# Two products moved in the hand-written order of a two-layer graph network: V's second and G's fourth

## The chip, the cores and the metric

The kernel runs on one core of a Trainium2 chip. The time is the device time of one execution in microseconds (us). The core has five engines with a queue of instructions each: PE (TensorE, matrix products), DVE (VectorE), ACT (ScalarE), POOL (GpSimd) and SP (SyncE, which here only issues DMAs). An engine works through its queue in order; where an instruction needs what another engine makes, or a buffer that another engine still reads, it waits on a semaphore, and all that is behind it in its queue waits too.

## The reference

The input `x` has 128 sets of 128 rows of 512 numbers, all float32. Two layers follow one another on it:

```python
# layer 0
h = jnp.maximum(_layernorm(x, axis=-1), 0.0)
x = x + _L0_gnn_ref(h, adj, L0_gnn_Wq, L0_gnn_Wk, L0_gnn_Wv)
# layer 1
h = jnp.maximum(_layernorm(x, axis=-1), 0.0)
x = x + _L1_gnn_ref(h, adj, L1_gnn_Wq, L1_gnn_bq, L1_gnn_Wk, L1_gnn_bk, L1_gnn_Wv, L1_gnn_bv)
```

Layer 0 makes `q`, `k` and `v` by three products with 512x512 weights, then `rel = adj.T * (q k^T)`, divides each row of `rel` by its norm, and returns `rel v`. Layer 1 is attention with 8 heads of 64: scores `q k^T / 8`, a mask from `adj`, softmax over each row, and the product with `v`.

## The kernel before

**Groups and layers.** Four of the 128 sets form a group (`G = 4`), so there are 32 groups. `run` (L707) goes through a list of step names, written out by hand, and calls each step in turn. A cycle of the main loop (L735 to L740) handles several groups at different stages at once: `m` is the group in layer 0, `n` the same group as it enters layer 1, `l` the group before it in layer 1, `p` and `o` those before that, `f` the next group, whose inputs are fetched. The lists are `FIRST` (cycle 0, L673), `SECOND` (cycle 1, L680), `ORDER` (cycles 2 to 31, L689: 30 cycles) and `LAST` (L699). The scheduling is manual (L720), so each engine gets its instructions in just the order in which the steps issue them.

**Products by seven.** Each big product (512 rows of a group by a 512x512 weight) is made as a 2x2 block product with seven block products instead of eight. `Product` (L202) has them as `P1` to `P7`. In layer 0 there are two: `G`, which takes the place of q and k together (`h` times the product of their weights), and `V`. In layer 1 there are `Q`, `K` and `V`. One `P` step issues four matmul calls, which are eight matmuls in the trace (x8 in a row), followed by one instruction of ACT or DVE that takes the result out of the accumulator memory (PSUM):

- `P1` fills bank "x"; ACT copies it out (`keep`).
- `P2` fills bank "y"; DVE adds it to what P1 left (`add`, L250).
- `P5` fills bank "z"; ACT copies it out.
- `P6` accumulates on "x"; ACT copies it out.
- `P3` accumulates on "z"; DVE adds it (`add`).
- `P7` accumulates on "x"; DVE adds it (`add`).
- `P4` accumulates on "x"; ACT copies it out.

So one bank x carries P1, P6, P7 and P4 in turn, and each time the result is read out before the next product accumulates on it. `V` of layer 1 uses DVE for all of them (`copy` with a bias row, L243). The names in the profile are `pg` (G), `pv` (V of both layers), `pq`, `pk`, with `_x`, `_y`, `_z` for the bank.

**Banks.** The banks of all products, and `po` of `A` (L625), come from one pool of four (`ps_mm`, L61). A bank is free for the next tile when the last reader of its old tile is done. V's "y" of layer 0 is special: after P2 is read out, `N` (L415) writes the row norms into the same bank, and `norms` (L425) reads them, so this bank stays taken from `m.V.P2` to `m.norms`.

**Inputs of the products.** `T` (L319) turns a half of `h` on DVE from what a DMA brought back (`u_h`). `sumA` and `sumB` (L357, L368) make the sums `s` of the blocks on DVE; G.P5 needs the first of them, and P6, P3 and P7 the others. `R` (L388) multiplies G's result with `h`, `mask_rel` applies the adjacency on DVE.

**The order around the change, in ORDER.** DVE's queue in this stretch holds `m.T1`, the two sums of `m.sumA`, `p.wt3` (a reciprocal and a transpose, L515 and L517), the two sums of `m.sumB`, the add of `m.G.P2`, those of `m.G.P3` and `m.G.P7`, `o.ot1` (L651: two transposes and two multiplications, whose results POOL adds to `out` by DMA), the add of `m.V.P2`, and the statistics of the next group (`f.stat0` to `f.stat3`). PE's queue holds K's last products, `m.G.P1`, `l.K.P4`, `m.G.P2`, `m.V.P1`, `m.G.P5`, `m.G.P6`, `m.G.P3`, `m.G.P7`, `m.V.P2`, `m.G.P4`, `m.V.P6`, `m.R`.

**The first two cycles.** FIRST takes group 1 (`f`) through all of G but P4, then turns layer 1's `h` of group 0 (`n.T0`), and SECOND begins with `l.Q.P1`, which needs it, then `m.G.P4` of group 1.

Of the kernel before, what the change touches and what calls it, by code (L numbers as in the profile page):

```python
# [21 lines left out]
def kernel(  # L22
# [352 lines left out]
    class Layer0(Layer):  # L375
        n = 0
# [64 lines left out]
    class Layer1(Layer):  # L441
        n = 1
# [232 lines left out]
        w.scale m.G.P3 m.V.P1 f.hn1 f.rd1 w.sumv m.G.P7 m.V.P2 w.sumq m.G.P4 m.V.P5  # L675
        m.R m.mask_rel m.square f.T0 m.V.P6 m.V.P3 m.N m.norms m.V.P7 m.O0 m.xO0 m.O1 m.xO1 n.stat0 n.stat1
        n.inv0 m.V.P4 n.hn0 n.rd0 f.T1 f.start f.G.P1 f.sumA m.O2 m.xO2 m.O3 m.xO3 n.stat2 n.stat3 n.inv1
        f.G.P5 f.sumB f.G.P6 n.hn1 n.rd1 f.G.P2 f.G.P3 f.G.P7 n.T0 w.sumk n.T1 n.start
    """.split()
    SECOND = """  # L680
        l.Q.P1 m.G.P4 l.sumA l.Q.P2 l.sumB l.K.P1 l.K.P2 l.Q.P5 l.Q.P6 l.sto0 l.sto1 f.load0 f.load1 l.Q.P3 l.K.P5 l.K.P6 l.Q.P7
        l.K.P3 l.K.P7 f.load2 f.load3 l.Q.P4 l.K.P4 m.V.P1 f.stat0 f.stat1 f.inv0
        m.V.P2 m.V.P6 m.R m.mask_rel m.square f.stat2 f.stat3 f.inv1
        l.S0 l.S1 m.N l.mkA1 m.norms m.V.P5 l.exC1 l.mkB1 m.V.P7 l.exD1 l.wr1 l.add_mask0 m.V.P3 l.mx0
# [4 lines left out]
    ORDER = """  # L689
        l.Q.P1 p.mkA3 l.sumA m.hn0 l.Q.P2 p.mkB3 l.K.P1 l.sumB m.rd0 l.K.P2 p.ot0 l.Q.P5 p.exC3 p.wt2 l.Q.P6 p.exD3 p.wr3  # L690
        m.hn1 m.rd1 l.sto0 l.sto1 l.Q.P3 l.Q.P7 m.T0 l.K.P5 l.K.P6 l.Q.P4 o.rdo1 f.load0 f.load1 l.K.P3
        l.K.P7 m.T1 m.sumA p.wt3 m.sumB m.start m.G.P1 l.K.P4 m.G.P2 f.load2 f.load3 m.V.P1 m.G.P5 m.G.P6
        m.G.P3 m.G.P7 o.ot1 m.V.P2 m.G.P4 f.stat0 f.stat1 f.inv0 f.stat2 f.stat3 f.inv1 m.V.P6 m.R m.mask_rel p.A1 m.square
        l.S0 p.oc1 l.S1 m.N l.mkA1 m.norms m.V.P5 l.exC1 l.mkB1 m.V.P7 l.exD1 l.wr1 l.add_mask0 m.V.P3 l.mx0
        m.V.P4 l.ex0 l.wr0 m.O0 m.xO0 m.O1 m.xO1 n.stat0 n.stat1 n.inv0 n.hn0 n.rd0 l.start_v l.V.P1 m.O2 m.xO2 m.O3 m.xO3
        n.stat2 n.stat3 n.inv1 l.V.P2 l.V.P5 n.hn1 n.rd1 l.wt1 l.V.P6
# [23 lines left out]
    with tc.manual_schedule(engines={EN.PE, EN.SP, EN.Pool, EN.DVE, EN.Activation}):  # L720
        o, p, l, m = None, None, None, Layer0(0)
# [9 lines left out]
        f = Layer0(1)  # L731
# [3 lines left out]
        for g in range(NG):  # L735
            n = Layer1(g)
            if g:
                f = Layer0(g + 1) if g + 1 < NG else None
            run((FIRST, SECOND, ORDER)[min(g, 2)], o=o, p=p, l=l, m=m, n=n, f=f, w=Weights1())
            o, p, l, m = p, l, n, f  # L740
# [31 lines left out]
```

## Time and profile before

| what | us |
|---|---|
| median of the runs shown (3) | 2475.11 (2472.4 to 2475.55) |
| the profiled execution | 2480.48 |
| its span, first to last instruction | 2478.7 |
| one cycle of ORDER, from V's P5 of one group to that of the next (1019.74 to 1095.78) | 76.0 |
| one product of eight matmuls, from its start to that of the next | 1.73 |
| an add of DVE from PSUM (L250) | 0.69 |
| a copy of ACT from PSUM (L234) | 0.585 |
| transpose of half of `h` on DVE (L322) | 1.24 |
| all waits of DVE for `u_h` (88 times) | 238.8 |
| waits of DVE for G's bank z, in all (31) and for G's bank x (32) | 69.8 and 32.0 |

Times in the profile count from the start of the span. In rows of the timeline and of the chain of waits the first number is the start and the second the length; x8 is the number of instructions merged into the row, and a bracket gives the idle time of the engine before it with what ended it. Matmuls are pipelined, so a group of eight shows 1.89 us in the timeline although the next begins 1.73 us after it. A window's row has, after its length, the busy time and number of instructions of PE, of PE's weight loads, DVE, ACT and POOL, then the granted clock of TensorE (1.00 is full), the DMA share and GB/s.

### The profile page before, as it was taken

How to read it: one execution, taken by the hardware profiler on the slowest of the kernel's cores; microseconds unless marked ns; L12 is line 12 of the kernel's file. 1: busy time of each engine (PE TensorE's matmuls, PEld its weight loads, DVE VectorE, ACT ScalarE, POOL GpSimd, SP SyncE). 2: the span in 40 equal slices, each digit the busy share in tenths (PEclk: the TensorE clock that was granted, in tenths of full speed). 3: DMA queues.
4: the chain of work that ended last, by engine and by line, in shares of the span. 5: the costliest groups of instructions: out<-in, count | busy, mean ns of one | idle time of the engine just before them, and what ended most of it. 6: DMA issues, size and time to landing. Idle time of an engine off the chain costs nothing.

```text
span 2478.7 us, 40450 instructions
## 1 busy us (share of the span) xinstructions
PE 2464.8 (99%) x14688; PEld 2117.4 (85%) x14688; DVE 1684.5 (68%) x2739; ACT 1012.4 (41%) x3248; POOL 375.9 (15%) x692
## 2 busy tenths in 40 slices
PE   9999999999999999999999999999999999999999
PEld 7888888888888888888888888888888888888887
DVE  6557776676766677766767666676667776676757
ACT  3334433444434344333444343443434434344434
POOL 5110111111111111111111111111111111111101
PEclk9999999999999999999999999999999999999999
DMA  5257656676566775566665667656677656676656
GB/s 190 96 163 204 176 166 177 170 202 195 161 174 170 192 208 163 166 178 174 204 180 169 177 169 199 193 161 175 170 195 205 168 164 177 172 205 180 169 153 162
DMA packets 396407, 438.20 MB, mean 177 GB/s; under 512 B 31600, under 2 KB 289008, under 8 KB 396208
## 3 DMA queue, kind: packets, MB, share of 16 engines
q1 hardware_dynamic: 297376, 201.22, 31.6%
q10 hardware_dynamic: 70000, 165.96, 18.1%
q0 software_dynamic: 28832, 68.44, 13.8%
q8 instruction: 116, 1.90, 0.3%
q14 instruction: 83, 0.68, 0.1%
HBM read 204.80 MB, written 230.69 MB: 176 GB/s over the span
## 4 chain that ended last, share of the span: by engine, by line
PE 90%; DVE 4%; DMA 3%; issue 1%; SPq 1%; ACT 1%; POOL 0%; DVEq 0%; POOLq 0%
PE pv_x L226 16%; PE pg_x L226 9%; PE pv_z L226 8%; PE pq_x L226 8%; PE pk_x L226 8%; PE pr L393 5%; PE pg_z L226 5%; PE po L634 4%; PE pq_z L226 4%; PE po L433 4%; PE pv_y L226 4%; PE pk_z L226 4%; PE pss L478 3%; PE pso L478 2%; PE pg_y L226 2%; PE pq_y L226 2%
## 5 line engine op out<-in xcount | busy, mean ns | idle before, releaser
L322 DVE STREAM_TRANSPOSE h<-u_h 128x1024 f32<-128x1024 f32 x126 | 156.6, 1243 | 249.0 <-DMA u_h<-d_h 238.8
L226 PE MATMUL pv_x<-wc_v,h 128*128 128x256 f32 x1280 | 305.9, 382 | 1.0 <-DVE v L243 1.0
L226 PEld LDWEIGHTS pv_x<-wc_v,h 128*128 128x128 f32 x1280 | 240.4, 190 | 52.0 <-issue 20.6
L668 POOL DMA_DIRECT2D out_dram<-o x124 | 110.4, 898 | 973.8 <-DVE o L661 931.8
L310 ACT ACTIVATE hn<-xb,shift,rstd 128x512 f32<-128x512 f32 x252 | 191.1, 807 | 149.6 <-POOL shift L302 114.7
L226 PE MATMUL pv_z<-wc_v,s 128*128 128x256 f32 x1024 | 245.2, 382 | 0.5 <-DVE v L243 0.5
L226 PEld LDWEIGHTS pv_z<-wc_v,s 128*128 128x128 f32 x1024 | 191.9, 190 | 31.9 <-issue 6.2
L234 ACT COPY gT<-pg_x 128x512 f32<-128x512 f32 x96 | 56.2, 585 | 360.6 <-PE pg_x L226 359.7
L226 PE MATMUL pq_x<-h,wc_q 128*128 128x256 f32 x768 | 183.0, 381 | 2.8 <-issue 2.0
L226 PE MATMUL pv_x<-wc_v,s 128*128 128x256 f32 x768 | 181.6, 379 | 0.0
L226 PE MATMUL pk_x<-h,wc_k 128*128 128x256 f32 x768 | 181.5, 379 | 0.0
L531 ACT ACTIVATE e<-pso,nmax 128x128 f32<-128x128 f32 x504 | 179.1, 392 | 2.5 <-DVE nmax L551 2.4
L291 DVE BATCH_NORM_STATS2 st<-xb 128x6 f32<-128x512 f32 x256 | 171.4, 670 | 8.5 <-DMA xb<-in_x_dram 8.5
L517 DVE STREAM_TRANSPOSE wT<-u_w 128x1024 f32<-128x1024 f32 x126 | 152.7, 1212 | 34.5 <-DMA u_w<-d_w 34.0
L226 PEld LDWEIGHTS pq_x<-h,wc_q 128*128 128x128 f32 x768 | 146.1, 191 | 24.4 <-issue 3.1
L226 PEld LDWEIGHTS pk_x<-h,wc_k 128*128 128x128 f32 x768 | 145.8, 190 | 20.0 <-issue 0.2
L226 PEld LDWEIGHTS pv_x<-wc_v,s 128*128 128x128 f32 x768 | 145.7, 190 | 20.0 <-issue 0.2
L645 ACT COPY oT<-po 128x512 f32<-128x512 f32 x124 | 72.0, 581 | 206.2 <-PE po L634 203.8
L548 DVE TENSOR_TENSOR pso<-pso,mask 128x512 f32<-128x512 f32 x128 | 87.2, 681 | 96.7 <-PE pso L478 96.7
L301 POOL TENSOR_TENSOR rstd<-rstd,mhalf 128x2 f32<-128x2 f32 x128 | 90.8, 709 | 379.0 <-DVE shift L300 379.0
L70 POOL DMA_DIRECT2D xb<-in_x_dram x124 | 68.7, 555 | 450.1 <-DMA out_dram<-xb 375.4
L234 ACT COPY v<-pv_x 128x512 f32<-128x512 f32 x96 | 56.2, 585 | 179.2 <-PE pv_x L226 179.2
(153 smaller groups left out, 4887.0 us busy)
## 6 DMA issues: line engine op xcount, KB each, us to landing
d_h<-hn ACTq DMA_DIRECT2D x126, 512.0 KB, 3.8
u_h<-d_h SPq DMA_DIRECT2D x504, 128.0 KB, 3.8
d_w<-e ACTq DMA_DIRECT2D x126, 512.0 KB, 3.4
u_w<-d_w SPq DMA_DIRECT2D x504, 128.0 KB, 3.3
out_dram<-xb SPq DMA_DIRECT2D x126, 256.0 KB, 4.0
xb<-in_x_dram POOLq DMA_DIRECT2D x124, 256.0 KB, 4.8
d_o<-oT ACTq DMA_DIRECT2D x62, 512.0 KB, 3.0
u_o<-d_o SPq DMA_DIRECT2D x248, 128.0 KB, 3.9
```

Source lines behind the costliest of these rows:

```text
L226: nc.tensor.matmul(ps[:, m, :], lhsT=lhsT, rhs=rhs, start=first and m == 0 and k == 0, stop=k == 1, skip_group_check=True,)
L234: nc.scalar.copy(to, ps)
L291: nc.vector.bn_stats(st, x_tiles[g, b])
L310: nc.scalar.activation(hn[:, r], x_tiles[g, b].rearrange("p (k j q) -> p j k q", j=TB, q=BK), AF.Relu, bias=self.shift[:, b : b + 1], scal ...
L322: nc.vector.transpose(half.rearrange("p k (t i) -> p t k i", i=BK), self.u.pop(i).rearrange("p t (k q) -> p t k q", q=BK),)
L393: nc.tensor.matmul(pr[:, b, :], lhsT=self.turned(k, b), rhs=self.gT[k // 2][:, k % 2, ts(b, P)], start=(k == 0), stop=(k == KD - 1),)
L433: nc.tensor.matmul(po, lhsT=self.rel[:, b, :], rhs=self.v[:, b, :], start=True, stop=True)
L478: nc.tensor.matmul(half[r][:, k, :], lhsT=self.qT[rows, k, ts(b, P)], rhs=self.kT[rows, k, ts(b, P)], start=True, stop=True,)
L517: nc.vector.transpose(self.wT[b].rearrange("p h (t i) -> p t h i", i=BK), self.uw.pop(b).rearrange("p t (h q) -> p t h q", q=BK),)
L531: nc.scalar.activation(e[:, :, i, :], sc[:, k, :].rearrange("p (j q) -> p j q", q=BK), AF.Exp, bias=nmax[:, i : i + 1], accum_out=self.tot ...
L634: nc.tensor.matmul(po[r * HD : (r + 1) * HD, k, :], lhsT=self.v[b // 2][:, b % 2, ts(2 * k + r, HD)], rhs=wT[:, r * NH + k, :], start=True ...
L668: nc.gpsimd.dma_start(out[g * G + b], o.rearrange("p k t q -> p (k t q)"), accum_op=ALU.add)
```

## The change

In ORDER, `m.V.P2` stands right behind `m.V.P1`, ahead of `m.G.P5`; before, it stood between `m.G.P7` and `m.G.P4` (with `o.ot1`, which has no work for PE). So `m.G.P7` and `m.G.P4` are now neighbours on PE. In the first two cycles, group 1's `G.P4` moves from SECOND, behind `l.Q.P1`, to the end of FIRST, ahead of it. In FIRST (`m`) and SECOND V's second product keeps its place. No step is added or dropped, and LAST is as before.

```diff
@@ FIRST
-        f.G.P5 f.sumB f.G.P6 n.hn1 n.rd1 f.G.P2 f.G.P3 f.G.P7 n.T0 w.sumk n.T1 n.start
+        f.G.P5 f.sumB f.G.P6 n.hn1 n.rd1 f.G.P2 f.G.P3 f.G.P7 n.T0 f.G.P4 w.sumk n.T1 n.start
@@ SECOND
-        l.Q.P1 m.G.P4 l.sumA l.Q.P2 l.sumB l.K.P1 l.K.P2 l.Q.P5 l.Q.P6 l.sto0 l.sto1 f.load0 f.load1 l.Q.P3 l.K.P5 l.K.P6 l.Q.P7
+        l.Q.P1 l.sumA l.Q.P2 l.sumB l.K.P1 l.K.P2 l.Q.P5 l.Q.P6 l.sto0 l.sto1 f.load0 f.load1 l.Q.P3 l.K.P5 l.K.P6 l.Q.P7
@@ ORDER
-        l.K.P7 m.T1 m.sumA p.wt3 m.sumB m.start m.G.P1 l.K.P4 m.G.P2 f.load2 f.load3 m.V.P1 m.G.P5 m.G.P6
-        m.G.P3 m.G.P7 o.ot1 m.V.P2 m.G.P4 f.stat0 f.stat1 f.inv0 f.stat2 f.stat3 f.inv1 m.V.P6 m.R m.mask_rel p.A1 m.square
+        l.K.P7 m.T1 m.sumA p.wt3 m.sumB m.start m.G.P1 l.K.P4 m.G.P2 f.load2 f.load3 m.V.P1 m.V.P2 m.G.P5 m.G.P6
+        m.G.P3 m.G.P7 o.ot1 m.G.P4 f.stat0 f.stat1 f.inv0 f.stat2 f.stat3 f.inv1 m.V.P6 m.R m.mask_rel p.A1 m.square
```

## The prediction

> **What bounds the kernel now.** I read the engine totals first, then the chain of waits, then one cycle of the order in the chain and in the timeline.
>
> ```profile
> PE 2464.8 (99%) x14688; PEld 2117.4 (85%) x14688; DVE 1684.5 (68%) x2739; ACT 1012.4 (41%) x3248; POOL 375.9 (15%) x692
> ...
> PE 90%; DVE 4%; DMA 3%; issue 1%; SPq 1%; ACT 1%; POOL 0%; DVEq 0%; POOLq 0%
> ```
>
> TensorE (PE) is busy all the time and is 90% of the chain. A busy PE could hide stretched matmuls, so here is one cycle of the chain, around the moved products:
>
> ```profile
> 1074.07 1.73 PE pv_x L226 x8
> 1075.79 1.81 PE pg_z L226 x8
> 1077.61 1.73 PE pg_x L226 x8
> 1079.33 1.73 PE pg_z L226 x8
> 1081.06 1.73 PE pg_x L226 x8
> 1082.79 1.73 PE pv_y L226 x8
> 1084.51 1.73 PE pg_x L226 x8
> ```
>
> The rows are V.P1, G.P5, G.P6, G.P3, G.P7, V.P2, G.P4. A product is eight matmuls at 0.216 us, 1.73 us, and each follows the last without a gap. There is almost no wait to win: between 100 and 2400 us the waits of PE sum to 3.8 us. The time is PE's work, and any wait that PE is newly given is added to it. So the question is which waits of PE the seven products above keep covered.
>
> The vector engine (DVE) in that cycle (start, length, then idle time before it and its releaser):
>
> ```profile
> 1073.52 1.25 DVE L322 STREAM_TRANSPOSE h<-u_h 128x1024 f32<-128x1024 f32 x1 [3.91 <-DMA u_h<-d_h]
> 1074.80 0.69 DVE L365 TENSOR_TENSOR s<-h 128x512 f32<-128x512 f32 x1
> ...
> 1076.25 1.19 DVE L517 STREAM_TRANSPOSE wT<-u_w 128x1024 f32<-128x1024 f32 x1
> ...
> 1078.54 0.68 DVE L250 TENSOR_TENSOR gT<-pg_y,gT 128x512 f32<-128x512 f32 x1
> ...
> 1082.82 0.69 DVE L250 TENSOR_TENSOR gT<-pg_x,gT 128x512 f32<-128x512 f32 x1 [0.96 <-PE pg_x L226]
> ```
>
> G.P2 left PE at 1073.9, but its bank y is read only at 1078.54 to 1079.22: DVE first does m.T1, which waits for a DMA, then sumA, p.wt3 and sumB. From the start of T1 to the end of that add it is 5.70 us in each of the 30 cycles that run ORDER.
>
> **The change, part by part.** No product is added or dropped: the 35 products of a group stay. Moved are V.P2 (eight matmuls and one DVE add) and G.P4 (eight matmuls and one ACT copy); neither issues a DMA, so SP's and POOL's queues keep their order.
>
> *V.P2 ahead of G.P5: banks.* The pool at line 61 has four banks. At G.P5 now, G's x, V's x and G's y are taken, and the fourth is the one that K.P4 left (its ACT copies end at 1073.2, long before). After the change V's y takes that fourth bank, and it stays taken until the norms are read from it. G.P5's z has then only the bank of G's y, and waits for the add of G.P2. The price per cycle: start of T1 + 5.70 + 0.06 (release to PE, below), less start of V.P1 + 3.45 (two products). Here 1073.52 + 5.76 - (1073.90 + 3.45) = 1.93 us. I took both starts from the timeline in all 30 cycles: 0.56 to 3.07 us, mean 1.65, sum 49.6. G.P5's present waits go, since V.P2 covers them or the new wait contains them: from start to start they sum to 4.2 us, nearly all of it in five cycles (0.3 to 1.2 us each). Net **+45.4**. Bounds: if the add of G.P2 were out of the way, -4.2; if T1 came 0.3 us later in each cycle, +54.
>
> *V.P2 no longer between G.P7 and G.P4.* Both accumulate into G's bank x, and the add of G.P7 must have read it before G.P4 writes. In all 30 cycles the add starts 0.20 us after PE has turned to V.P2 and ends at +0.89; V.P2's 1.73 us hid that. Now G.P4 follows at once and stands still. The nearest row is at the end of the program, where V.P7 meets a bank that DVE is still reading:
>
> ```profile
> 2460.89 0.68 DVE L243 TENSOR_TENSOR v<-pv_x,bv_sb 128x512 f32<-128x512 f32 x1
> ...
> 2461.63 1.99 PE L226 MATMUL pv_x<-wc_v,h 128*128 128x256 f32 x8 [1.00 <-DVE v L243]
> ```
>
> The add ends at 2461.57 and PE starts 0.06 us later. So 0.89 + 0.06 = 0.95 us, 30 times: **+28.6**. Behind the waiting G.P4 stand V.P6 and R, and the whole of PE's order. From below: the wait can't be under the add's own 0.69 us (+20.7); from above, 1.2 us if DVE is late (+36). I take the row, since DVE idles 0.96 us before this add.
>
> *Restart.* After each wait of G.P5 in this trace the first matmul takes 0.29 us where 0.216 is normal. 60 waits less the 6 visible now, by 0.075: **+4.1**.
>
> *G.P4 in the first cycle, ahead of Q.P1.* Now G.P7 ends at 64.93, Q.P1 waits for n.T0 until 67.07, and Q.P1 and G.P4 end at 72.29. After: add of G.P7 to 65.82, G.P4 from 65.88 to 67.69, then Q.P1, whose transpose is done at 66.97, to 69.42. **-2.9**, carried on, since the next sums from the DMA (s, 72.17) are there before Q.P5 asks at 74.6. If they were late, between -2.9 and 0.
>
> *What I cost at nothing.* mask_rel: DVE idles 1.57 us before it now. After, between G.P7's end and R's end lie 0.95 + 0.08 + 1.73 + 1.73 + 3.67 = 8.2 us; DVE needs 0.89 + 2.7 (ot1) + 3.2 (stats) = 6.8, so it still waits. G.P4's ACT copy has V.P6 ahead of R as before. V.P2's add now stands behind G.P2's add on a DVE that then idles 1.95 us. ot1's two stores on POOL slip with the waits, and PE does not wait for them.
>
> *The clock.* The windows view, with the granted clock (PEclk) as third value from the end:
>
> ```profile
> 64.27:67.68 3.41, 1.43 (x7) 0.97 (x6) 2.52 (x4) 0.00 (x0) 0.00 (x0) 1.00 0.42 144
> 67.68:71.09 3.41, 3.41 (x10) 2.69 (x9) 2.68 (x4) 0.81 (x2) 0.00 (x0) 0.50 0.97 320
> 2371.68:2375.09 3.41, 2.44 (x12) 1.85 (x11) 3.34 (x5) 0.58 (x1) 0.00 (x0) 1.00 0.90 244
> 2375.09:2378.51 3.42, 3.42 (x17) 3.02 (x16) 2.00 (x4) 1.17 (x2) 0.00 (x0) 1.00 0.01 4
> ```
>
> These windows are a grid of 3.41 us on which the clock changed. In the first PE is busy for 1.43 us, and the next runs at half clock (1.7 us lost); in the third it is busy for 2.44, and nothing follows. From start to start of the matmuls, whose ends are modelled, PE was idle for 2.1 and 1.1 us. The Trainium skill, "TensorE: Matmul & The Clock Gate", section "Why this matters for your kernels", asks only that no idle gap exceed some 3 us. By that rule two of my waits (3.07 and 3.04) at most slow the clock, 0 to +3.4. By the row the limit is somewhere between 1.1 and 2.1 us idle in one window; with waits at random against the grid, 21 windows are slowed at the lower end and 3 at the upper. I take half a window, 1.7 us: 7 windows by 1.71, **+12**; both ends (+5, +37) go to the range. A wait of 0.95 us slows none.
>
> Sum: 45.4 + 28.6 + 4.1 - 2.9 + 12 = **+87**. The profiled execution took 2480.5 (span 2478.7 and 1.8 around it), so 2567.7; it lies 5.4 above the median of the runs shown, 2475.1, so the runs should show **2562 us**, 3.5% more.
>
> **The rivals.**
> *A, the clock slows in most cycles* (limit near 1.1 us idle): 2475.1 + 75.2 + 37 = 2587; were half of the 0.95 us waits to trip it too, another 26. For: no row between 1.1 and 2.1 us. Against: the two windows with over 1.1 us idle that kept full speed. 0.13.
> *B, only the wait at G.P4.* If G.P2's add is done when G.P5 asks, or a bank is free, 28.6 + 2.3 (restarts) - 4.2 and their 0.5 of restarts - 2.9 = +23, 2498 us. For: the banks can't be seen in the profile. Against: by counting what is live, no bank is left, and the 5.70 us of DVE are in each cycle. 0.11.
> *C, not slower.* The place is G.P5: V.P2 covers its wait for s (4.2 us), and the first cycle gives 2.9: -7, 2468 us. It decides where bank x is free for G.P4 within 7/30 = 0.24 us of G.P7's end and G.P5 finds a bank; the add alone is 0.69. 0.03. That the order does not change what PE does is excluded, since PE runs it as written.
>
> **How the numbers follow.** The forecast, both waits with a few slow clock windows, 0.73: 2535 to 2585, as T1's start against V.P1 moves by a few tenths of a us with the DMA. With A the range goes to 2602; B stays out: 2530 to 2602. Slower 0.96; faster 0.025 (C); within 0.2%, about what runs of this kernel can tell, 0.015.
>
> **What would show it.** In the profile after: PE waits for pg_z on DVE's gT of line 250, 30 times, 1.65 us in the mean; pg_x of G.P4 starts 0.95 us after G.P7's stream ends, on the same line; PEclk windows of 0.50 after the longest waits alone; no 2 us gap near 65. It is wrong if G.P5 starts without a wait (B), if half-clock windows number over 15 (A), or if T1 moves against V.P1 once the cycle is longer.

## The result, and the profile after

| kernel | median of runs, us | lowest to highest |
|---|---|---|
| before | 2475.33 (4 runs) | 2472.4 to 2477.78 |
| changed | 2536.79 (4 runs) | 2534.52 to 2540.8 |

The ratio on record is 1.0253, 95% interval 1.0241 to 1.0265; the medians differ by 61.5 us. The prediction was 2562, a cost of 87, with a range from 2530 to 2602. The direction was right and so were the places. The size was 25 us too large, and the measured time lies near the lower edge of the range.

The page of the changed kernel, the engines' totals and the chain of waits:

```profile
PE 2477.4 (98%) x14688; PEld 2113.0 (83%) x14688; DVE 1684.4 (67%) x2739; ACT 1014.1 (40%) x3248; POOL 376.9 (15%) x692
...
PE 67%; DMA 12%; DVE 8%; issue 5%; SPq 4%; ACT 3%; POOL 0%; DVEq 0%; ACTq 0%; POOLq 0%
```

PE has the same 14688 matmuls. Its share of the chain fell from 90% to 67%, though PE itself is still at 98%: the chain now leaves PE twice in a cycle, once through DVE's queue to the DMAs ahead of T1 and once for the add of G.P7. The share of busy time shows next to nothing of the change, while the chain shows where it is.

What PE waits for in the whole span of the changed kernel (total, times, longest):

```profile
PE pg_x L226 <- DVE gT L250: 24.3, 31, 0.8
PE pg_z L226 <- DVE gT L250: 24.0, 24, 2.1
```

Neither row was there before. The first is G.P4 behind the add of G.P7, 30 times in ORDER and once in the first cycle. The second is G.P5 behind the add of G.P2. From start to start of the matmuls the sums are 29.3 and 29.5 us, since the rows count from the modelled end of the last matmul, and short waits fall out of the second.

Part of one cycle of the chain of waits after (start, length, what), and below it T1 and V.P1 of the same cycle from the timeline:

```profile
1099.92 0.65 DVE s L369
1100.57 0.60 DVE s L370
1101.17 0.61 DVE gT L250
...
1101.83 1.99 PE pg_z L226 x8
1103.82 1.73 PE pg_x L226 x8
1105.55 1.73 PE pg_z L226 x8
1107.27 1.74 PE pg_x L226 x8
...
1109.04 0.70 DVE gT L250
...
1109.78 1.99 PE pg_x L226 x8
```

```profile
1096.07 1.25 DVE L322 STREAM_TRANSPOSE h<-u_h 128x1024 f32<-128x1024 f32 x1 [2.77 <-DMA u_h<-d_h]
...
1097.60 1.89 PE L226 MATMUL pv_x<-wc_v,h 128*128 128x256 f32 x8
```

The chain comes to G.P5 (1101.83) through DVE: T1 (1096.07), which waited for the DMA of `u_h`, the rows after it down to sumB's two, then G.P2's add. It stays with PE for four products, leaves it for the add of G.P7 (1109.04), and returns to G.P4. By the prediction's formula G.P5 starts at 1096.07 + 5.76 = 1101.83, which is what the row has.

### The profile page after: what moved, and what is told of

The parts are those of the page before. It is cut to its first block, busy times and chain, and to the rows that moved or that the text cites. A ratio compares the mean times of both kernels' runs of the same rounds, so it can differ in the third digit from the quotient of the medians.

```text
span 2532.7 us, 40390 instructions
## 1 busy us (share of the span) xinstructions
PE 2477.4 (98%) x14688; PEld 2113.0 (83%) x14688; DVE 1684.4 (67%) x2739; ACT 1014.1 (40%) x3248; POOL 376.9 (15%) x692
## 3 DMA queue, kind: packets, MB, share of 16 engines
q0 software_dynamic: 28832, 68.44, 13.1%
## 4 chain that ended last, share of the span: by engine, by line
PE 67%; DMA 12%; DVE 8%; issue 5%; SPq 4%; ACT 3%; POOL 0%; DVEq 0%; ACTq 0%; POOLq 0%
PE pv_x L226 14%; PE pv_z L226 8%; PE pg_x L226 7%; DMA u_h<-d_h 5%; PE pg_z L226 5%; PE pr L393 5%; PE po L634 4%; PE po L433 4%; DMA d_w<-e 4%; SPq L199 3%; PE pq_x L226 3%; PE pk_x L226 3%; PE pss L478 2%; PE pq_z L226 2%; ACT e L531 2%
## 5 line engine op out<-in xcount | busy, mean ns | idle before, releaser
L226 PE MATMUL pg_z<-s,wc_a 128*128 128x256 f32 x512 | 124.6, 386 | 24.6 <-DVE gT L250 24.0
L226 PE MATMUL pg_x<-h,wc_a 128*128 128x256 f32 x512 | 124.2, 385 | 24.3 <-DVE gT L250 24.3
```

The lines of the kernel that those rows point to most:

```text
L226: nc.tensor.matmul(ps[:, m, :], lhsT=lhsT, rhs=rhs, start=first and m == 0 and k == 0, stop=k == 1, skip_group_check=True,)
```

## The experiments

Each was run beside the kernel before on the same chip, in three sets. In the first set (only the first cycle, neighbours, bank, longer cycle) and in the third (the last four expectations below) the kernel before took 2475.08 us, in the second 2480.19. "T1 was 1.30 ahead" means that T1 started 1.30 us before V.P1. This lead, and the time from a DMA's issue to its landing, are taken from the trace, as a mean over the cycles of ORDER (28 or 29 of the 30). The edits are shown against the changed kernel, with `...` for steps left out.

**Only the first cycle changed.** ORDER as before:

```diff
-        ... m.V.P1 m.V.P2 m.G.P5 m.G.P6
-        m.G.P3 m.G.P7 o.ot1 m.G.P4 f.stat0 ...
+        ... m.V.P1 m.G.P5 m.G.P6
+        m.G.P3 m.G.P7 o.ot1 m.V.P2 m.G.P4 f.stat0 ...
```

> ORDER is as before, only G's fourth product of group 1 stands ahead of the first Q.P1. If the two waits in ORDER make up the loss, this has none of it: 2.9 us less than before (0.12%), about 2472 us, with the half-clock window near 68 us gone. Rival, that a later DMA takes the gain back: 2475. T1 against the start of V.P1 was 0.62 us ahead in the mean before and 1.33 us ahead after the change. If the longer cycle moved it, it is 0.6 ahead here again; if single executions differ that much, it may be anything up to 1.3.

Measured 2473.01 (21 runs), ratio 0.9990, 0.9984 to 0.9997: 2.1 us less. T1 was 1.30 ahead of V.P1, not 0.6, and the waits for s came to 0.3 us, not 4.2, in an ORDER that is just that of the kernel before. So the longer cycle isn't what moved T1.

**Neighbours at G.P4, without the bank.**

```diff
-        ... m.V.P1 m.V.P2 m.G.P5 m.G.P6
-        m.G.P3 m.G.P7 o.ot1 m.G.P4 f.stat0 ...
+        ... m.V.P1 m.G.P5 m.G.P6
+        m.G.P3 m.G.P7 o.ot1 m.G.P4 m.V.P2 f.stat0 ...
```

> V.P2 behind G.P4: G.P7 and G.P4 are neighbours as in the change, but G.P5 is asked for as before, with the bank of K free. If the two waits are separate, PE waits 0.95 us at G.P4 in 30 cycles with 0.075 of restart each, and nowhere at G.P5 on the add of G.P2: 28.4 + 2.3 - 2.9 = +28, about 2503 us. If all of the loss comes from the bank at G.P5, it is 2472. If a cycle that is 1 us longer draws T1 ahead, T1 is 0.8 us or more ahead of V.P1 and the waits for s (4.2 us) shrink: 2500.

2504.73, ratio 1.0120 (1.0106 to 1.0134): 29.7 us more. The wait table of PE has the wait at G.P4 as before it stood, and none at G.P5 on the add of G.P2:

```profile
PE pg_x L226 <- DVE gT L250: 24.3, 31, 0.8
...
PE pg_z L226 <- DVE s L365: 0.4, 1, 0.4
```

**The bank, without the neighbours.** V.P6 stands between G.P7 and G.P4:

```diff
-        m.G.P3 m.G.P7 o.ot1 m.G.P4 f.stat0 f.stat1 f.inv0 f.stat2 f.stat3 f.inv1 m.V.P6 m.R ...
+        m.G.P3 m.G.P7 o.ot1 m.V.P6 m.G.P4 f.stat0 f.stat1 f.inv0 f.stat2 f.stat3 f.inv1 m.R ...
```

> The change with V.P6 put between G.P7 and G.P4: the add of G.P7 is covered again, the wait for G.y's bank stays. If the waits are separate: no wait at G.P4, 30 waits at G.P5. With T1 as after the change (29.5 us of waits): 29.5 + 2.3 - 4.7 - 2.9 = +24, about 2499 us. With T1 as before, because the cycle is shorter by the 0.95 us: 45.4 + 2.3 - 2.9 = +45, about 2520. If all of the loss were at G.P4: 2468.

2506.04, ratio 1.0118 (1.0102 to 1.0135): 31.0 us more. Its waits of PE:

```profile
PE pg_z L226 <- DVE gT L250: 26.2, 27, 1.9
...
PE pg_x L226 <- DVE gT L250: 0.8, 1, 0.8
```

T1 was 1.28 ahead and the wait at G.P5 31.1 us from start to start. The 2499 expected for this place of T1 was 7 short: it took off waits for s (4.7 with their restarts) that are not there when T1 is early. Without this wrong credit it is 2504. The two waits are separate and add: 29.7 + 31.0 + 2.1 (both have the first cycle's gain in them) = 62.8, against 61.5 for the change.

**A longer cycle.** The kernel before, with R's loop run twice (`for b in (*range(G), *range(G))`).

> The kernel before, with the products of R made twice over in each of the 32 groups, which makes each cycle 3.57 us longer on PE alone behind G.P4 and changes no wait by itself: +114, about 2589 us. If a longer cycle gives the DMAs ahead of T1 more room, T1 comes 1.3 us or more ahead of V.P1 in the mean instead of 0.62, the write of d_w lands in 5.6 us or less instead of 6.2, and the waits of G.P5 for s (4.2 us) go: 2585. If the cycle's length has nothing to do with it: T1 0.6 ahead, d_w 6.2 us, 2589.

2586.80, ratio 1.0453 (1.0439 to 1.0468). T1 was 1.36 ahead. `d_w`, the write of layer 1's weights to memory that ACT issues just before `d_h`, landed 5.75 us after its issue (`d_h` is what T1's `u_h` is read back from). Taken alone this fits the theory of the longer cycle, but the kernel with only the first cycle changed has no longer cycle and T1 at 1.30, in the same set.

**The kernel before, profiled again,** in the second set.

> The kernel before, unchanged, profiled a second time. If the first profile of it was an execution in which the DMAs ahead of T1 were late, T1 comes about 1.3 us ahead of V.P1's start in the mean (0.61 in the first profile), d_w lands 5.8 us after its issue (6.2 in the first), the waits of G.P5 for s are under 1 us in all (4.2 in the first) and the execution takes about 2475 us, not 2480. If it is the order of the kernel before that delays T1, all of these are as in the first profile.

2477.26 in one run, beside 2480.19. T1 was 0.69 ahead, d_w landed after 6.11 us, and the waits for s came to 3.9: as in the first profile. This alone would say that the order of the kernel before delays T1. But in this second set all four kernels had T1 at 0.7 to 0.8, whatever their order, and in the other two sets all had 1.27 to 1.41 but one that changes a DMA. One and the same program, the version with both waits covered (below), had T1 0.76 ahead in the second set and 1.31 in the third. So T1's place goes with the set of runs, not with the order. The chip alone does not explain it as far as the record goes, which gives the second and the third set the same chip number.

**The queue ahead of the add.** In the second set, p.wt3 alone, then p.wt3 and m.sumB, behind G.P2's add:

```diff
-        ... m.sumA p.wt3 m.sumB m.start m.G.P1 l.K.P4 m.G.P2 f.load2 ...
+        ... m.sumA m.sumB m.start m.G.P1 l.K.P4 m.G.P2 p.wt3 f.load2 ...
```

> The change with p.wt3 (1.31 us of DVE) moved behind the add of G.P2, nothing else. If the wait of G.P5 is the queue of DVE ahead of that add, it shrinks by 1.31 us in each cycle down to nothing: from 29.5 to about 3.5 us in all, and with a third as many restarts the time falls by 27 us, to about 2509. If G.P5 waits for something else, the time stays at 2537.

2521.88, ratio 1.0171 (1.0157 to 1.0185). The wait at G.P5 was 15.1 us. The numbers expected were for T1 at 1.3; here it was 0.78. Also, taking p.wt3 out shortens T1 to add from 5.70 to 4.62, by 1.08 and not 1.31, since its rows overlap with their neighbours. With both put right, the formula gives 15.3 from this run's T1. So the mechanism holds, and the expectation missed by its inputs.

```diff
-        ... m.sumA p.wt3 m.sumB m.start m.G.P1 l.K.P4 m.G.P2 f.load2 ...
+        ... m.sumA m.start m.G.P1 l.K.P4 m.G.P2 p.wt3 m.sumB f.load2 ...
```

> The change with p.wt3 and m.sumB (2.49 us of DVE) moved behind the add of G.P2. If the wait of G.P5 is that queue, none is left in any cycle, and only the 30 waits at G.P4 remain: as with V.P2 behind G.P4, about 2504 us. If P3 or P7 then wait for the sums that sumB makes later, it is more, up to 0.7 us per cycle, 2525.

2504.56, ratio 1.0101 (1.0087 to 1.0115): 24.4 more than the 2480.19 beside it. The wait at G.P5 is down to 1.2 us in three cycles, and the 30 waits at G.P4 are there in full.

**Both covered.** This edit of the sums and V.P6 ahead of G.P4 together, run in the second and the third set, and in the third beside the version with only the first cycle changed.

> The change with p.wt3 and m.sumB behind the add of G.P2, and with V.P6 between G.P7 and G.P4: both waits covered, V.P2 still ahead of G.P5. If these two waits are all that the change costs, the time is that of the kernel with only the first cycle changed, 2473 us, or 1 us under it where G.P5's last waits for s are covered: 2472. If V.P2's early place costs something of its own (its bank held longer, its add in DVE's queue), it is above 2480.

> Only the first cycle changed, as before in another set of runs: 2 to 3 us less than the kernel before. It stands here beside the version with both waits covered. If V.P2's early place is worth the waits for s that it covers, that version is faster than this one by them: under 1 us where T1 comes 1.3 us ahead, about 4 us where it comes 0.7 ahead.

> V.P2 early with both waits covered, a second time: 7 us less than before where the kernel before takes 2480 and T1 comes 0.7 us ahead, 2 to 3 us less where it takes 2475 and T1 comes 1.3 us ahead.

Second set: 2473.23 beside 2480.19, ratio 0.9974 (0.9965 to 0.9983). Third set: 2470.19 beside 2475.08, ratio 0.9980 (0.9972 to 0.9988), and only the first cycle changed 2472.54, ratio 0.9992 (0.9985 to 0.9998). One cycle of its chain in the third set:

```profile
1070.32 1.73 PE pv_x L226 x8
1072.05 1.73 PE pv_y L226 x8
1073.78 1.73 PE pg_z L226 x8
1075.50 1.73 PE pg_x L226 x8
1077.23 1.73 PE pg_z L226 x8
1078.95 1.73 PE pg_x L226 x8
1080.68 1.73 PE pv_x L226 x8
1082.41 1.73 PE pg_x L226 x8
```

V.P1, V.P2, G.P5, G.P6, G.P3, G.P7, V.P6, G.P4: V.P2 stands where the change put it, and PE doesn't leave the chain. This version beats both kernels, by 4.9 to 7.0 us against the one before. So V.P2's early place shows no cost of its own once both waits are covered. Its lead of 2.4 us over the first cycle alone is more than the 0.1 us of waits for s that were left in that run. The two profiled executions are only 0.7 us apart (2471.38 and 2470.68), so they cannot show where the rest comes from; it stays open.

**The change once more, and ot0's stores.**

> The change, unchanged, once more. In two sets of runs so far the kernel before took 2475 and 2480 us, and T1 came 1.3 and 0.7 us ahead of V.P1. If T1's place belongs to the chip and sets the price at G.P5: beside a before of 2475, 2537 again with T1 1.3 ahead and 29 us of waits at G.P5; beside a before of 2480, T1 0.7 to 0.8 ahead, some 46 us of waits, a few windows at half clock, and 2480 + 72 to 77 = 2552 to 2557. If the price is the same everywhere: 62 more than before in both.

2535.67 beside 2475.08, ratio 1.0244 (1.0230 to 1.0258): T1 1.41 ahead, 27.7 us of waits at G.P5. The set was one with T1 early, so the other half of this expectation was not tried.

In the last kernel ot0's two stores are plain writes, which leaves the residual out of the output for the first two sets of each group:

```diff
-                nc.gpsimd.dma_start(out[g * G + b], o.rearrange("p k t q -> p (k t q)"), accum_op=ALU.add)
+                more = {"accum_op": ALU.add} if i else {}
+                nc.gpsimd.dma_start(out[g * G + b], o.rearrange("p k t q -> p (k t q)"), **more)
```

> The change, with ot0's two stores of a group as plain writes instead of adds in memory (the first two sets of each group lose the residual in the output; the work of the engines is the same). These stores go out 2 us ahead of the write of d_w, which T1 waits for through d_h. If they share the DMA engines with it and so set the place of T1, d_w lands at least 1 us sooner than in the same set's run of the change, T1 moves ahead by as much, and the waits of G.P5 fall by some 25 us of their 29 to 46. If T1's place comes from something else: d_w as in the change, and the time within 3 us of it.

2509.67, ratio 1.0137 (1.0121 to 1.0152): 26.0 us less than the change beside it. d_w landed 4.39 us after its issue instead of 5.62, d_h 3.79 instead of 5.15, and T1 came 2.58 ahead instead of 1.41. PE's waits on the add of G.P2 nearly went:

```profile
PE pg_z L226 <- DVE gT L250: 3.2, 4, 1.6
```

From start to start these waits fell from 27.7 us to 4.7. So two stores of the output, issued by POOL in another part of the cycle, decide most of how long PE waits for a PSUM bank. As adds they let d_w and d_h land later, `u_h` can then be read back only later, T1 starts 0.12 us after `u_h` has landed, and the add of G.P2 follows T1. POOL's DMA queue with the adds, and with plain writes in their place (packets, MB, share of the span of the 16 DMA engines):

```profile
q0 software_dynamic: 28832, 68.44, 13.1%
```

```profile
q0 software_dynamic: 24864, 68.44, 11.1%
```

For the same bytes that is some 53 us less of all 16 engines (13.1% of 2530.6 less 11.1% of 2509.1), or 1.7 us for each of the 31 groups that issue these stores, as an estimate. This fits stores that take up DMA engines which d_w and d_h need. It was not separated from other ways in which an add could hold them up. In the first profile of before, and in the second set, d_w took 6.1 to 6.2 us; why is open.

## Why the prediction was right in kind and too large

| term | predicted | measured |
|---|---|---|
| wait at G.P5 for the bank of G's y | +49.6 | +29.5 |
| waits for s that go | -4.2 | -0.3 (from the first cycle's version) |
| wait at G.P4 for the add of G.P7 | +28.6 | +28.4 (30 by 0.947) |
| restarts | +4.1 | +6.2 (60 by 0.104) |
| first cycle | -2.9 | -2.1 and -2.5 |
| half clock | +12 | +1.7 (one window; none in the second profile) |
| sum | +87 | 63; the runs say +61.5 |

**Right: the two places, their mechanism and the formula.** Four banks leave G.P5 only that of G's y; the distance from T1 to the end of the add is 5.70 in the changed kernel too; PE starts 0.05 to 0.06 us after it. With the changed kernel's own T1 the formula gives 29.7 us. The row from the end of the program was the right price for G.P4. Rival B, one wait only, is refuted by the two halves; rival A, the clock, by the count of windows.

**The step that missed: "I took both starts from the timeline in all 30 cycles ... mean 1.65".** T1's start was taken from one execution and treated as the kernel's. It comes at the end of a chain of DMAs, and 0.7 us of it per cycle, in the mean, goes with the set of runs: 0.65 ahead in the first profile of before, 1.32 in that of the change. The profiled execution took 2480.5 us when the runs shown took 2472 to 2476; the prediction noted this and only took the 5.4 us off the sum. The difference was a sign that something in it was late, and the term that depends on a DMA was the place to widen. That term is 20 us too large, against an error of 25 in all. The half clock is 10 too large (next paragraph); the waits for s, from the same late T1, give 4 back, and the restarts 2. The prediction worked out a price for a T1 that comes later (+54) but none for one that comes earlier, and named a T1 that moves as a sign of being wrong. T1 did move, though not because the cycle is longer: by 0.67 us, where the range allowed for a few tenths. So it is in part luck that the result still fell into the range. What makes T1 late stays open.

**The limit for the clock was set too low.** Windows of the changed kernel, then of the kernel before in its second profile (length, PE busy, PE's weight loads, DVE, ACT, POOL, granted clock, DMA share, GB/s):

```profile
393.72:397.13 3.41, 1.43 (x7) 1.16 (x7) 2.66 (x5) 0.00 (x0) 0.00 (x0) 1.00 0.96 323
397.13:400.54 3.41, 3.41 (x10) 2.67 (x9) 0.00 (x0) 0.59 (x1) 0.00 (x0) 0.50 0.00 1
```

```profile
62.77:66.18 3.41, 1.50 (x7) 0.97 (x6) 2.44 (x4) 0.00 (x0) 0.00 (x0) 1.00 0.42 159
66.18:69.59 3.41, 3.33 (x16) 2.98 (x17) 2.63 (x5) 0.84 (x2) 0.00 (x0) 1.00 0.98 280
```

With 1.43 us busy the next window is at half clock, with 1.50 it is not. From start to start of the matmuls, PE stood idle from 393.71 to 395.84 in the first case, 2.12 us of it in the window, and from 64.11 to 66.26 in the second, 2.07 us of it in the window. The prediction took half a window, 1.7 us, as the limit; in these windows it lies between 2.07 and 2.12 us, the upper end of its bounds. The rule that the prediction weighed, gaps of some 3 us, is too lenient here: 2.12 us within one window was enough. But at +3.4 us at most it came nearer to the measured +1.7 than the half window did.

**The first cycle** gave less than its row. The new order has no gap there:

```profile
62.32 1.89 PE L226 MATMUL pg_x<-s,wc_a 128*128 128x256 f32 x8
64.99 1.99 PE L226 MATMUL pg_x<-h,wc_a 128*128 128x256 f32 x8 [0.78 <-DVE gT L250]
66.82 1.89 PE L226 MATMUL pq_x<-h,wc_q 128*128 128x256 f32 x8
68.55 1.89 PE L226 MATMUL pq_y<-h,wc_q 128*128 128x256 f32 x8
```

From G.P7 to Q.P2 it is 6.23 us, 2.9 less than the 9.1 in the first profile of before, just as worked out. In the second profile of before the gap is the same but reaches into the next window, no half clock follows, and the stretch takes 7.4. The gain is 2.9 in one execution and 1.2 in another.

## What to carry to other kernels

Before a product is moved forward, count the banks that are live at its new place: the product that asks after it gets what is left, and pays for whatever stands in the reader's queue ahead of the read that frees it. Before a product is moved away, look at what it covered: two products that accumulate on one bank, with a read of DVE between them, needed about 1 us of other work between them here. Where the price hangs on a DMA's landing, one profile gives it to no better than the spread of that landing; a profiled execution that lies outside the range of the runs is a warning about just these terms.

## What was not expected

Changing two adds in memory (256 KB each, per group) to plain writes shortened the write of d_w that follows 2 us later from 5.6 to 4.4 us. And the same program with the same 2.15 us gap ran on at half clock in one execution and at full clock in another, by where the gap fell on the grid of 3.41 us.
